# Strassen on the second MLP product of a fused vision-tower kernel, with one layernorm result moved from VectorE to ScalarE

## The chip, the core and the metric

The kernel runs on one core of a Trainium2 chip. The core has a matrix engine (TensorE, written PE), three engines for elementwise work (VectorE or DVE, ScalarE or ACT, GpSimd or POOL), a queue engine (SyncE or SP), an on-chip memory (SBUF), and a small memory into which PE alone accumulates and which the other engines read (PSUM[...]). Each engine works through its own list of instructions in order; semaphores hold an instruction back until what it depends on is done. The metric is the device time of one execution in microseconds (us), lower is better.

## What is computed

The reference, cut to what matters here. Everything is fp32. There are 16384 tokens of 256 features, which the kernel works through in 32 blocks of 512 tokens.

```python
h = tokenizer(x, L0_tok_W)                    # patches, rfft, one matmul: (tokens, 256)
x = layernorm(h)                              # "the first layernorm's result", needed for the residual
# --- attention layer (retention) on x
g = layernorm(x, ln1_g, ln1_b)
q, k, v = g @ Wq.T + bq, g @ Wk.T + bk, g @ Wv.T + bv
mem_t = decay * mem_(t-1) + k_t * v_t         # a scan over the tokens
x = x + q * mem
h2 = layernorm(x, ln2_g, ln2_b)
mlp = relu(h2 @ W1.T + b1) @ W2.T + b2        # 256 -> 1024 -> 256; the second product is changed
h = h + x + mlp
# --- mixture of experts on layernorm(h): 8 experts, each token goes to 2 of them
tok = layernorm(h)
logits = tok @ router_w.T                     # softmax, top 2
h = h + tok + sum over the 2 experts e of share_e * (gelu(tok @ w1[e] + b1[e]) @ w2[e] + b2[e])
```

## The kernel before

Three blocks are in work at once: in one pass of the main loop the newest block (`new`) is embedded and goes through retention, the one before it (`mid`) goes through the MLP, and the one before that (`old`) is routed to its experts. Between these parts stand "slots": in each slot one tile of 256 tokens of some expert is worked on (`enter` is its first matrix product, `leave` its second, `sums` the scaling and the scatter of its result). The order of the instructions on PE, DVE, ACT and SP is that in which the program gives them.

```python
p_mm = ... tile_pool(name="p_mm", bufs=4, PSUM)    # 4 buffers of one bank
p_tm = ... tile_pool(name="p_tm", bufs=3, PSUM)    # 3 buffers
p_sm = ... tile_pool(name="p_sm", bufs=1, PSUM)    # 1 buffer
...
class Norm:
    def apply(self, dst, src, i=0):                # (src - mean) * rstd, on DVE
        for t in range(TT):                        # TT = 4
            nc.vector.tensor_scalar(dst[:, t, :D], src[:, t, :], self.mv[:, t, 0:1],
                                    self.rstd[:, i, t : t + 1], ALU.subtract, ALU.mult)
...
def embed(self):                                   # the end of it
    ...
    norm.factors(twice=True)                       # rstd, on GpSimd
    yield
    self.z = one.tile([P, TT, D], F32, name="z")
    self.zz = one.tile([P, TT, D], F32, name="zz")
    norm.apply(self.zz, self.h, 1)                 # both layernorms in one
    norm.apply(self.z, self.h, 0)                  # the first layernorm, for the residual
...
def residual(self):
    norm = Norm()
    for u in range(U):                             # U = 2
        ps = p_tm.tile([P, 2, D], F32, name="tm")
        ...                                        # 4 transposes of ret into ps, on PE
        nc.vector.tensor_tensor(self.z[:, ts(u, 2), :], ps, self.z[:, ts(u, 2), :], ALU.add)
        for i in range(2):
            norm.stats(self.z, 2 * u + i)
    norm.factors_here()                            # rstd, on DVE: small operations
    self.zz = one.tile([P, TT, D], F32, name="zz")
    norm.apply(self.zz, self.z)
...
def mlp_out(self, u, between=None):
    if u == 0:
        self.norm = Norm()
    ps = p_tm.tile([P, 2, D], F32, name="tm")
    for i in range(2):
        if i and between:
            between()
        for k in range(KH):                        # KH = 8
            nc.tensor.matmul(ps[:, i, :], lhsT=self.aT[:, k, ts(u * 2 + i, P)], rhs=w2_sb[:, k, :],
                             start=k == 0, stop=k == KH - 1)
    nc.vector.tensor_tensor(self.h[:, ts(u, 2), :], ps, self.h[:, ts(u, 2), :], ALU.add)
    for i in range(2):
        self.norm.stats(self.h, u * 2 + i)
    if u == U - 1:
        self.norm.factors_here() if self.i >= NS - 1 else self.norm.factors()
        self.tok = one.tile([P, TT, D], F32, name="tok")
        self.norm.apply(self.tok, self.h)
        ...
...
def sums(self):                                    # of an expert's tile
    ...                                            # 2 small operations for its share
    nc.vector.tensor_tensor(y, ps, bias, ALU.add)  # reads the p_tm buffer of leave
    for c in range(2):
        nc.vector.tensor_scalar(y[:, c, :], y[:, c, :], share[:, c : c + 1], None, ALU.mult)
    ...                                            # scatter-add by GpSimd's DMA queue
...
# the second part of one pass of the main loop
for m in range(KH):
    mid.mlp_in(m)                                  # relu(h2 @ W1.T + b1): aT
    if m == 1:
        new.split1()                               # zz to 16-bit planes, for a transposing DMA
    if m == TT - 1:
        slot(known)
    if m == KH - 3:
        blocks[i + 1].differences(xs.pop(i + 1))
        new.features1()                            # hT, for retention
for t in range(TT):
    old.logits(t)
for m in range(KD):                                # KD = 2
    new.retention(m)
    if old and m == 0:
        old.choose()
take(old.i + 1, old, old.place())                  # routing: small operations on DVE
...
slot(known)
mid.mlp_out(0)
new.residual()
slot(known)
new.split2()
mid.mlp_out(1)
# then the next pass: embed, slot, mlp_in of the next block
```

Of the kernel before, what the change touches and what calls it, by code (L numbers as in the profile page):

```python
# [12 lines left out]
F32 = mybir.dt.float32  # L13
I32 = mybir.dt.int32
# [21 lines left out]
def vit_tower_kernel(  # L36
# [21 lines left out]
    KD, KH = D // P, H // P  # L58
    J = STRIDE // 2
# [90 lines left out]
    w2_sb = const.tile([P, KH, D], F32)  # L150
    nc.sync.dma_start(out=w2_sb, in_=w2.rearrange("(k p) d -> p k d", p=P))
# [157 lines left out]
    class Block:  # L309
# [32 lines left out]
        def embed(self):  # L342
# [40 lines left out]
            self.z = one.tile([P, TT, D], F32, name="z")  # L383
            self.zz = one.tile([P, TT, D], F32, name="zz")
            norm.apply(self.zz, self.h, 1)
            norm.apply(self.z, self.h, 0)

        def split1(self):
            if self.i < EARLY:
                return  # L390
            self.turn = Turn()
            self.turn.split(self.zz)

# [89 lines left out]

        def mlp_out(self, u, between=None):
            if u == 0:
                self.norm = Norm()
            ps = p_tm.tile([P, 2, D], F32, name="tm")
            for i in range(2):
                if i and between:
                    between()  # L490
                for k in range(KH):
                    nc.tensor.matmul(  # L492
                        ps[:, i, :],
                        lhsT=self.aT[:, k, ts(u * 2 + i, P)],
                        rhs=w2_sb[:, k, :],
                        start=k == 0,
                        stop=k == KH - 1,
                    )
            nc.vector.tensor_tensor(self.h[:, ts(u, 2), :], ps, self.h[:, ts(u, 2), :], ALU.add)
            for i in range(2):  # L500
                self.norm.stats(self.h, u * 2 + i)
            if u == U - 1:
                self.norm.factors_here() if self.i >= NS - 1 else self.norm.factors()
                self.tok = one.tile([P, TT, D], F32, name="tok")
                self.norm.apply(self.tok, self.h)
                if self.i == NS:
                    nc.vector.tensor_tensor(self.h, self.h, self.tok, ALU.add)
                    return
                mean, rstd = self.norm.mv[:, :, 0], self.norm.rstd[:, 0, :]
                self.by = small.tile([P, 2, TT], F32, name="by")  # L510
                nc.vector.tensor_scalar(self.by[:, 0, :], rstd, 1.0, None, ALU.add)
# [672 lines left out]
```

## Time and profile before

| | |
|---|---|
| time, median of 3 runs | 2197.89 us (2197.12 to 2201.64) |
| span of the profiled execution | 2216.1 us |
| mean granted PE clock | 0.991 of full speed |
| PE busy | 98% of the span |
| DVE busy | 74% |
| ACT busy | 37% |
| POOL busy | 39% |
| chain of work that ended last | 88% of it on PE |

The profile is of one execution on the chip. A group is a set of instructions of one line, engine and operation, with the time that they were busy, the mean of one in nanoseconds, and the idle time of the engine before them with what ended it. A timeline gives instructions in order of time, neighbours of one kind merged: start, duration, engine, line, operation, what is written from what, how many, and in square brackets the idle time before and its releaser. PE's matmuls overlap in their ends, so the distance of their starts tells their pace, and the duration of one doesn't. LDWEIGHTS is the loading of a matmul's stationary operand.

### The profile page before, as it was taken

Reading aid. Unit: us, or ns where it says so; the run is one execution under the profiler, and the core shown is the slowest. Engines: PE = TensorE matmul, PEld = TensorE weight load, DVE = VectorE, ACT = ScalarE, POOL = GpSimd, SP = SyncE. Lnnn points to the kernel's source line nnn. Section 1 sums busy time; section 2 is a strip of 40 time slices with the busy share of each in tenths; the row PEclk is TensorE's granted clock in tenths of the full one; section 3 lists DMA queues with packets and bytes.
Section 4 is the critical chain, followed back from the end, with each engine's and each line's share of the span. In section 5 each row is a group of like instructions: output and inputs, shape, how many; then the busy total and the mean of one; then the engine's idle time right before and its main releaser. Section 6 shows DMA issues by size and latency. Waiting matters only on the chain.

```text
span 2216.1 us, 28920 instructions
## 1 busy us (share of the span) xinstructions
PE 2161.2 (98%) x8548; PEld 1544.3 (70%) x8548; DVE 1650.9 (74%) x5150; ACT 825.6 (37%) x1329; POOL 873.1 (39%) x760
## 2 busy tenths in 40 slices
PE   8999999999999999999999999999999999998999
PEld 6666666667676667777666777666677766676676
DVE  6678877778778777877877777777787777766454
ACT  1223323444334443432444432344443334442443
POOL 0022243344444434444434444443444444344444
PEclk9999999999999999999999999999999999999999
DMA  3022265676565677657567656665765666588743
GB/s 135 20 97 75 79 147 125 134 163 122 127 149 135 143 139 150 125 129 155 129 139 149 135 128 135 149 136 132 163 130 130 138 146 137 115 172 205 116 66 45
DMA packets 425389, 284.95 MB, mean 129 GB/s; under 512 B 355216, under 2 KB 391056, under 8 KB 421136
## 3 DMA queue, kind: packets, MB, share of 16 engines
q1 hardware_dynamic: 374304, 210.21, 41.4%
q0 software_dynamic: 49632, 67.39, 16.1%
q10 hardware_dynamic: 1296, 5.52, 1.0%
q8 instruction: 67, 1.10, 0.2%
q14 instruction: 90, 0.74, 0.1%
HBM read 118.36 MB, written 88.39 MB: 93 GB/s over the span
## 4 chain that ended last, share of the span: by engine, by line
PE 88%; DVE 3%; DMA 3%; ACT 3%; issue 2%; another core or an unknown queue 0%; POOL 0%; ACTq 0%; DVEq 0%; SPq 0%; POOLq 0%
PE mm L298 31%; PE tm L492 19%; PE tm L353 11%; PE mm L799 9%; PE tm L816 9%; DMA turned<-planes 3%; PE sm L557 2%; PE tm L888 1%; PE tm L451 1%; PE mm L871 1%; PE mm L131 1%; PE mm L265 1%; ACT h L518 1%; ACT row L533 1%; ACT hT L292 1%
## 5 line engine op out<-in xcount | busy, mean ns | idle before, releaser
L839 POOL DMA_INDIRECT out<-y,xg x262 | 429.3, 1638 | 501.0 <-DVE y L835 225.9
L492 PE MATMUL tm<-w_sb,aT 128*128 128x256 f32 x2048 | 462.3, 380 | 16.5 <-issue 14.6
L298 PE MATMUL mm<-hT,w_sb 128*128 128x512 f32 x1024 | 455.4, 596 | 10.7 <-ACT ge L807 5.7
L492 PEld LDWEIGHTS tm<-w_sb,aT 128*128 128x128 f32 x2048 | 387.2, 190 | 80.8 <-issue 27.1
L298 PEld LDWEIGHTS mm<-hT,w_sb 128*128 128x128 f32 x1024 | 193.9, 191 | 232.6 <-issue 207.6
L298 PE MATMUL mm<-hT,wqkv_sb 128*128 128x512 f32 x768 | 342.5, 602 | 4.2 <-DVE hT L292 4.2
L640 POOL DMA_INDIRECT xbuf<-row,to x248 | 242.3, 977 | 258.8 <-DVE full L699 182.4
L807 ACT ACTIVATE ge<-mm,w 128x256 f32<-128x256 f32 x262 | 109.3, 469 | 574.3 <-issue 525.8
L353 PE MATMUL tm<-wu,xv 128*128 128x256 f32 x1280 | 284.8, 381 | 0.0
L298 PEld LDWEIGHTS mm<-hT,wqkv_sb 128*128 128x128 f32 x768 | 145.3, 192 | 176.4 <-issue 160.4
L353 PEld LDWEIGHTS tm<-wu,xv 128*128 128x128 f32 x1280 | 244.3, 191 | 33.3
L799 PE MATMUL mm<-xT,w 128*128 128x256 f32 x1048 | 251.3, 383 | 1.5 <-DVE tile_share L828 1.5
L816 PE MATMUL tm<-w,ge 128*128 128x256 f32 x1048 | 247.6, 379 | 0.9 <-DVE y L833 0.9
L482 ACT ACTIVATE aT<-mm,vec 128x512 f32<-128x512 f32 x256 | 169.9, 684 | 173.7 <-PE mm L298 170.5
L799 PEld LDWEIGHTS mm<-xT,w 128*128 128x128 f32 x1048 | 195.6, 191 | 38.6 <-issue 13.1
L816 PEld LDWEIGHTS tm<-w,ge 128*128 128x128 f32 x1048 | 199.0, 190 | 31.3 <-issue 3.4
L792 ACT COPY xT<-xh 128x512 uint16<-128x512 uint16 x262 | 181.2, 761 | 5.4 <-DMA xh<-xbuf 5.3
L243 POOL TENSOR_SCALAR rstd<-mv 128x4 f32<-128x4 f32 x62 | 41.6, 671 | 319.2 <-DVE mv L224 317.3
L833 DVE TENSOR_TENSOR y<-tm,w 128x512 f32<-128x512 f32 x131 | 90.6, 692 | 70.5 <-PE tm L816 69.7
L416 ACT ACTIVATE ks<-mm,vec 128x512 f32<-128x512 f32 x64 | 44.0, 687 | 248.6 <-PE mm L298 248.6
L597 POOL TENSOR_TENSOR ex<-euler,second 128x4 f32<-128x4 f32 x32 | 34.7, 1084 | 247.1 <-DVE second L589 247.1
L418 DVE SCALAR_TENSOR_TENSOR kv<-mm,vec,ks 128x512 f32<-128x512 f32 x64 | 47.9, 748 | 108.9 <-PE mm L298 108.9
(155 smaller groups left out, 2498.2 us busy)
## 6 DMA issues: line engine op xcount, KB each, us to landing
w<-in_wex SPq DMA_DIRECT2D x113, 641.5 KB
xb<-in_x SPq DMA_DIRECT2D x32, 1040.0 KB
out<-h SPq DMA_DIRECT2D x31, 512.0 KB
bank<-in_wex ACTq DMA_DIRECT2D x8, 641.5 KB
out<-y,xg POOLq DMA_INDIRECT x262
xbuf<-row,to POOLq DMA_INDIRECT x248
xh<-xbuf SPq DMA_TRANSPOSE x131
xg<-xbuf SPq DMA_DIRECT2D x131, 4.0 KB
```

Source lines behind the costliest of these rows:

```text
L298: nc.tensor.matmul(ps, lhsT=w[:, k, ts(m, P)], rhs=rhs[:, k, :], start=k == 0, stop=k == KD - 1)
L353: nc.tensor.matmul(ps[:, n, :], lhsT=xv[:, i, j, :], rhs=wu[:, i, j, :], start=j == 0, stop=j == J - 1)
L418: nc.vector.scalar_tensor_tensor(own_order(self.kv[:, m, :]), tiles_order(pv), vec[:, BV + m : BV + m + 1], own_order(ks), ALU.add, ALU.mult,)
L482: nc.scalar.activation(self.aT[:, m, :], ps, AF.Relu, bias=vec[:, MB1 + m : MB1 + m + 1])
L492: nc.tensor.matmul(ps[:, i, :], lhsT=self.aT[:, k, ts(u * 2 + i, P)], rhs=w2_sb[:, k, :], start=k == 0, stop=k == KH - 1,)
L640: write = nc.gpsimd.indirect_dma_start(out=xbuf, out_offset=bass.IndirectOffsetOnAxis(ap=to[:, c, t : t + 1], axis=0), in_=self.row[:, t, ...
L792: nc.scalar.copy(halves[:, :, :, 1 - i], self.xh[:, i * KD : (i + 1) * KD, :])
L799: nc.tensor.matmul(ps[:, m, :], lhsT=self.w[:, k * D + m * P : k * D + (m + 1) * P], rhs=self.xT[:, k, :], start=k == 0, stop=k == KD - 1,)
L807: nc.scalar.activation(self.ge[:, m, :], ps[:, m, :], AF.Gelu, bias=self.w[:, 5 * D + m : 5 * D + m + 1])
L816: nc.tensor.matmul(ps[:, c, :], lhsT=self.ge[:, k, ts(c, P)], rhs=w[:, (2 + k) * D : (3 + k) * D], start=k == 0, stop=k == KD - 1,)
L833: nc.vector.tensor_tensor(y, ps, w[:, 4 * D : 5 * D].unsqueeze(1).to_broadcast([P, 2, D]), ALU.add)
L839: add = nc.gpsimd.indirect_dma_start(out=out, out_offset=bass.IndirectOffsetOnAxis(ap=self.xg[:, c, NUMBER - D : NUMBER - D + 1], axis=0), ...
```

## The change

The second MLP product, for one block, is a (512 x 1024) times (1024 x 256) product. It is cut into quarters: the activations A into A11, A12 (first 256 tokens) and A21, A22 (last 256), each with half of the 1024 inner columns; the weights B into B11, B12, B21, B22. The plain way needs eight products of quarters. The change uses Winograd's form of Strassen's method with seven: A11 B11, A12 B21, A22 T4, S2 T2, S1 T1, S3 T3, S4 B22. The combinations T1 to T4 of the weights are formed once. The combinations S1 to S4 of the activations are formed by DVE in each block, and the seven results are added into the four quarters of `h`. Its purpose is to take one eighth of this product's multiplications from PE.

So that DVE gets something back, the first layernorm's result for the residual (`z`) is computed by ACT, as scale times `h` plus bias. To make room in SBUF some buffers are made single (`row`, `past`, `table_f`), and the S combinations lie in buffers of other tiles that are free at that time.

The diff, cut to its core:

```diff
-    w2_sb = const.tile([P, KH, D], F32)
+    w2_sb = const.tile([P, 7, KQ, P], F32)        # KQ = 4
...
-            self.z = one.tile([P, TT, D], F32, name="z")
             self.zz = one.tile([P, TT, D], F32, name="zz")
             norm.apply(self.zz, self.h, 1)
-            norm.apply(self.z, self.h, 0)
+            self.norm1 = norm
...
+        def result1(self):
+            mean, rstd = self.norm1.mv[:, :, 0], self.norm1.rstd[:, 0, :]
+            less = small.tile([P, TT], F32, name="less")
+            nc.vector.scalar_tensor_tensor(less, mean, -1.0, rstd, ALU.mult, ALU.mult)
+            self.z = one.tile([P, TT, D], F32, name="z")
+            for t in range(TT):
+                nc.scalar.activation(self.z[:, t, :], self.h[:, t, :], AF.Identity,
+                                     bias=less[:, t : t + 1], scale=rstd[:, t : t + 1])
...
+        def combine1(self):
+            self.A11, self.A12 = [self.aT[:, i * KQ : (i + 1) * KQ, : BLK // 2] for i in range(2)]
+            self.A21, self.A22 = [self.aT[:, i * KQ : (i + 1) * KQ, BLK // 2 :] for i in range(2)]
+            shape = [P, KQ, BLK // 2]
+            self.S1 = one.tile(shape, F32, name="tok")
+            self.S2 = one.tile(shape, F32, name="tokT")
+            self.S3 = self.A21
+            nc.vector.tensor_tensor(self.S1, self.A21, self.A22, ALU.add)
+            nc.vector.tensor_tensor(self.S2, self.S1, self.A11, ALU.subtract)
+            nc.vector.tensor_tensor(self.S3, self.A11, self.A21, ALU.subtract)
+
+        def combine2(self, place):
+            self.S4 = one.tile([P, KQ, BLK // 2], F32, name=place)
+            nc.vector.tensor_tensor(self.S4, self.A12, self.S2, ALU.subtract)
...
+            def product(to, a, b):
+                for i in range(2):
+                    for k in range(KQ):
+                        nc.tensor.matmul(to[:, i, :], lhsT=a[:, k, ts(i, P)], rhs=w2_sb[:, b, k, :],
+                                         start=k == 0, stop=k == KQ - 1)
+            def add(to, what):
+                nc.vector.tensor_tensor(to, to, what, ALU.add)
+            h = self.h.rearrange("p (a i) (c d) -> p a c i d", i=2, d=P)
+            U = self.aT[:, 0, : BLK // 2].rearrange("p (i d) -> p i d", d=P)
             if u == 0:
+                self.ps = p_sm.tile([P, 2, 2, P], F32, name="sm")
+                product(self.ps[:, 0], self.A11, B11)
+                nc.scalar.copy(U, self.ps[:, 0])
+                add(h[:, 0, 0], U)
+                return
+            if u == 1:
+                ps = p_tm.tile([P, 2, 2, P], F32, name="tm")
+                product(ps[:, 0], self.A12, B21)
+                if between:
+                    between()
+                product(ps[:, 1], self.A22, T4)
+                add(h[:, :, 0], ps)
+                return
+            product(self.ps[:, 1], self.S2, T2)
+            add(U, self.ps[:, 1])
+            add(h[:, 0, 1], U)
+            product(self.ps[:, 0], self.S1, T1)
+            add(h[:, :, 1], self.ps[:, 0].unsqueeze(1).to_broadcast([P, 2, 2, P]))
+            if between:
+                between()
+            ps = p_tm.tile([P, 2, 2, P], F32, name="tm")
+            product(ps[:, 0], self.S3, T3)
+            add(U, ps[:, 0])
+            add(h[:, 1], U.unsqueeze(1).to_broadcast([P, 2, 2, P]))
+            product(ps[:, 1], self.S4, B22)
+            add(h[:, 0, 1], ps[:, 1])
+            self.norm = Norm()
+            for t in (2, 3, 0, 1):
+                self.norm.stats(self.h, t)
...
-            self.row = two.tile([P, TT, RW], I32, name="row")
+            self.row = one.tile([P, TT, RW], I32, name="row")
... # the main loop
+                if m == 2:
+                    new.result1()
...
+            if mid:
+                mid.combine1()
             for m in range(KD):
                 new.retention(m)
...
             if old:
                 take(old.i + 1, old, old.place())
+            if mid:
+                mid.combine2("kv")
...
             slot(known)
             if mid:
                 mid.mlp_out(0)
             new.residual()
+            if mid:
+                mid.mlp_out(1)
             slot(known)
...
                 new.split2()
             if mid:
-                mid.mlp_out(1)
+                mid.mlp_out(2)
```

## The prediction

> **What bounds the kernel now.** I read the busy times first, then the groups by line, then one steady block in order of time, on TensorE (PE) and VectorE (DVE). The page's part 1 (busy us, share of the span, instructions):
>
> ```profile
> PE 2161.2 (98%) x8548; PEld 1544.3 (70%) x8548; DVE 1650.9 (74%) x5150; ACT 825.6 (37%) x1329; POOL 873.1 (39%) x760
> ```
>
> PE is busy 98% of the span, and the chain that ended last is 88% PE. So PE sets the end, and DVE seems to have a quarter to spare. That average misleads, as the order of time shows. Groups by line (busy us, mean ns of one, then idle before it):
>
> ```profile
> L492 PE MATMUL tm<-w_sb,aT 128*128 128x256 f32 x2048 | 462.3, 380 | 16.5 <-issue 14.6 <-DVE h L499 1.7
> L492 PEld LDWEIGHTS tm<-w_sb,aT 128*128 128x128 f32 x2048 | 387.2, 190 | 80.8 <-issue 27.1 <-DVE h L499 2.1
> L462 DVE TENSOR_TENSOR h<-h,z 128x1024 f32<-128x1024 f32 x32 | 38.2, 1193 | 0.0
> ```
>
> The first two are the product that is changed: each fp32 matmul leaves two records, so 1024 instructions are 2048. The third gives the price of a DVE addition of 1024 columns. Now one block, the PE's timeline from the start of retention (start, us, operation, count, idle before):
>
> ```profile
> 1011.50 10.54 PE L298 MATMUL mm<-hT,wqkv_sb 128*128 128x512 f32 x24 [0.79 <-DVE hT L292]
> ...
> 1022.23 1.97 PE L799 MATMUL mm<-xT,w 128*128 128x256 f32 x8
> 1024.04 1.89 PE L816 MATMUL tm<-w,ge 128*128 128x256 f32 x8
> 1025.77 7.07 PE L492 MATMUL tm<-w_sb,aT 128*128 128x256 f32 x32
> 1032.68 1.04 PE L451 MATMUL tm<-ident,ret 128*128 128x128 f32 x8
> 1033.55 1.89 PE L799 MATMUL mm<-xT,w 128*128 128x256 f32 x8
> 1035.28 1.89 PE L816 MATMUL tm<-w,ge 128*128 128x256 f32 x8
> 1037.01 7.27 PE L492 MATMUL tm<-w_sb,aT 128*128 128x256 f32 x32
> 1044.11 8.80 PE L353 MATMUL tm<-wu,xv 128*128 128x256 f32 x40
> ```
>
> And DVE in the same stretch:
>
> ```profile
> 1023.25 1.10 DVE L436 SCALAR_TENSOR_TENSOR ret<-mm,vec,ks 128x512 f32<-128x512 f32 x1
> ...
> 1030.21 0.15 DVE L735 TENSOR_TENSOR taken<-taken,upto 1x8 f32<-1x8 f32 x1
> ...
> 1030.65 0.69 DVE L833 TENSOR_TENSOR y<-tm,w 128x512 f32<-128x512 f32 x1
> ...
> 1032.88 0.69 DVE L499 TENSOR_TENSOR h<-tm,h 128x512 f32<-128x512 f32 x1 [0.88 <-PE tm L492]
> ...
> 1041.09 1.38 DVE L252 TENSOR_SCALAR zz<-z,mv,rstd 128x256 f32<-128x256 f32 x4
> ...
> 1050.01 1.38 DVE L252 TENSOR_SCALAR tok<-h,mv,rstd 128x256 f32<-128x256 f32 x4 [3.80 <-POOL rstd L248]
> ```
>
> From 1024.2 to 1030.4 DVE runs the routing of the block before (place and take: about 32 small operations, most near 0.2 us apart). PE doesn't notice, because the first half of the old product (7 us) needs nothing from DVE. From 1034.69 to 1042.47 DVE runs the residual and its layernorm in 7.8 us, and PE again has a slot (3.5) and the second half (7) to chew on. So in this stretch DVE is nearly full and runs one PE stage behind. Its idle time lies elsewhere: 3.3 us at the first `kv`, 3.8 and 1.8 us waiting for GpSimd's `rstd`, 0.9 here. Retention starts follow each other by 65.0 us (361.4 to 1921.1 for 24 blocks), and PE stands idle under 2 us of it.
>
> [...] 32 records of 256 columns from 1025.77 to 1032.68 are 216 ns each; transposes of 128 columns (8 in 0.87 us) are 109 each; and the router's 128x8 matmuls (16 in 1.8) take about 112[...]. [...] The new one puts two products into a bank and reads between them.
>
> **The change, part by part.** *PE.* 32 matmuls of 256 columns a block become 7 x 8 = 56 of 128. Before: 64 records x 216 ns = 13.8 us. After: 112 x 110 (or 112) = 12.3 to 12.5. So 1.4 us a block, 32 blocks, 45 us: the whole prize, and it is 2% of the run.
>
> *DVE.* Added per block: four operand combinations of 1024 columns, 4 x 1.2 = 4.8. The adds of the results: five of 256 columns (0.39 each, as L379) and three of 512 (0.69, L499), 4.0. Removed: two L499 (1.4) and the layernorm's second result (four L252, 1.38), which goes to ACT at about 2 us, with room at 37%. Net about +6 us a block, 190 us in all: DVE would be near 85%.
>
> *Path.* In the built program the waits are: the products of A12 and A22 write the `tm` buffer that the expert's `y` (old L833) must first have read; the S1 product waits for DVE's add of the S2 product (same bank), and the S4 product for the add of the S3 product (same bank). I walk a block from retention's start, times in us, durations from the lines above.
>
> DVE: the `hT` copies end at 0.5, three combinations at 4.1; the first `kv` could start at 3.8, so +0.4. `ret` ends at 13.1 (12.7 before). Place and take, 6.15: 19.25. S4, 1.2: 20.45. Shares 0.35 and `y` 0.7: 21.5. PE meanwhile: slot ends at 14.3, first product (free of `sm` at 14.35) at 16.1, transposes at 17.0. It now needs the `tm` buffer and gets it at 21.55: **4.5 us idle**. The cause is that only 1.8 us of product, not 7, lies there to cover place and take.
>
> PE: two products, 3.5: 25.05; slot, 3.45: 28.5; S2 product, 1.76: 30.3. DVE: `y` scaling 0.6, add 0.4: 22.5; residual 7.75: 30.25; add 0.7, shares and `y` 1.65, then the add that frees the bank 0.4: 33.0. S1 product starts at 33.05: **2.75 idle**. S1 and S3 end at 36.55; drain and one add about 0.6 later the last product starts, **0.6 idle**, and ends at 38.9. The old kernel starts the embedding at 32.6: the new one **6.3 later**, although it did 1.4 us less work.
>
> Behind it nothing gives this back. Four stats now all follow the last add (2.2 instead of 1.1 us), GpSimd's 3.8 us follows, so `tok` slips by 6.8 and the next layernorm with it; PE's own work from the embedding to the next retention is unchanged at 31.1. Next retention: about 38.9 + 31.1 + 1 = 71 instead of 65.0. **+6 us x 25 full blocks = +150.** The four blocks before them (periods of 51 to 58 us, no or few experts to fill PE) lose more at the same waits, some 7 each: +28. The tail, with expert steps between the parts: about 0 to +5. Sum: 2198 + 150 + 28 + 3 = 2379; some of the slip may be absorbed, so I say **2370**.
>
> **Rivals.** *PE stays the bound.* DVE has 25% idle and GpSimd waits could shrink as DVE falls behind; then 2198 - 45 = 2150. For it: PE at 98%, DVE at 74%. Against: the idle time isn't where the new work is; from retention to the last add DVE has almost none. *Only the bank round trips cost.* If DVE kept up, two stalls of about 0.6 us a block eat 40 of the 45 us: 2195. It needs the 4.5 us stall to be absent, which takes DVE being 4 us earlier. *Weight loading doesn't hide.* [...] Against: with 256 columns the loads lie wholly under the matmuls; transposes at 109 have a shorter load (141 against 190 ns), so they prove it only in part. The point of no gain is 13.8/112 = 123 ns.
>
> **Range and chances.** The walk needs two stalls with firm causes; even half of each makes +2 us a block after the saving, 2250. The upper side holds more waits that I didn't see, and early blocks worse than thought. Range 2290 to 2440. Faster by over 2% (below 2154) needs PE to stay the bound entirely: 0.03. Within 2%: 0.07. Slower: 0.90.
>
> **What would show it.** Right: PE busy drops by some 45 us or more while the span grows; in a steady block PE idles 4 to 5 us before the A12 product with DVE `y` as releaser, 2 to 3 before S1 and 0.6 before S4 with DVE `aT` adds; retention's distance is near 71; DVE near 1840 busy. Wrong: records of the 128-column product further apart than 115 ns, block distance below 66, or the PE wait ended by ACT or DMA rather than DVE.

## The result, and the profile after

The changed kernel takes 2398.22 us (median of 4 runs, 2391.55 to 2403.06); before took 2198.14 beside it (2197.12 to 2201.64). The ratio is 1.0905, with a 95% interval of 1.0876 to 1.0934. It is slower by 9%, inside the predicted range of 2290 to 2440 and 28 us above the predicted 2370.

Part 1 of the page after (busy us, share of the span, instructions), and the first line of its chain of work that ended last:

```profile
PE 2196.2 (92%) x10084; PEld 1622.2 (68%) x10084; DVE 1838.6 (77%) x5378; ACT 904.6 (38%) x1489; POOL 918.6 (38%) x760
...
PE 51%; DVE 42%; issue 3%; POOL 1%; DMA 1%; ACT 1%; DVEq 0%; SPq 0%; ACTq 0%; POOLq 0%
```

DVE carried 3% of the chain before and carries 42% now, at a busy share that rose only from 74% to 77%. PE does an eighth less of the product and is yet busy 35 us longer (2161.2 before). Both need the order of time. The PE timeline of one steady block, from the start of retention (start, us, operation, count, idle before and its releaser; A11 lies at 1127.55):

```profile
1112.90 10.55 PE L311 MATMUL mm<-hT,wqkv_sb 128*128 128x512 f32 x24
...
1134.47 5.47 PE L534 MATMUL tm<-w_sb,aT 128*128 128x128 f32 x32 [4.03 <-DVE y L908]
...
1145.76 2.05 PE L534 MATMUL sm<-w_sb,tok 128*128 128x128 f32 x16 [0.57 <-DVE aT L543]
...
1150.11 2.05 PE L534 MATMUL tm<-w_sb,kv 128*128 128x128 f32 x16 [0.51 <-DVE aT L543]
1152.00 8.80 PE L366 MATMUL tm<-wu,xv 128*128 128x256 f32 x40
```

The three stalls of the prediction are there: 4.03 before A12 and A22 (both merged in the second line), 0.57 before S1, 0.51 before S4. The embedding, last line, starts 39.1 after retention; in the block of before that the prediction shows it was 32.6. Over the 25 full blocks the means are 39.2 and 33.4. DVE in the same stretch:

```profile
1125.19 1.10 DVE L463 SCALAR_TENSOR_TENSOR ret<-mm,vec,ks 128x512 f32<-128x512 f32 x1
...
1132.25 1.21 DVE L525 TENSOR_TENSOR kv<-aT,tokT 128x1024 f32<-128x1024 f32 x1
...
1133.73 0.69 DVE L908 TENSOR_TENSOR y<-tm,w 128x512 f32<-128x512 f32 x1
...
1145.29 0.41 DVE L543 TENSOR_TENSOR aT<-aT,sm 128x256 f32<-128x256 f32 x1
...
1156.24 1.38 DVE L265 TENSOR_SCALAR tok<-h,mv,rstd 128x256 f32<-128x256 f32 x4 [1.49 <-POOL rstd L261]
```

None of the first four has a wait in brackets: DVE goes through routing, S4 (the `kv` line, in that buffer), `y`, residual and the adds without a gap, and the add at 1145.29, which frees the S1 bank, comes when the list has come so far. The second stall is shorter than predicted because A12 and A22 took 5.3 us from start to start of the next product, not 3.6. The view by stretches (us; busy us of PE, PEld, DVE, ACT, POOL with instructions; PE clock; DMA share; GB/s) of the stall and the time right behind it:

```profile
1130.20:1134.40 4.20, 0.24 (x3) 0.01 (x1) 3.92 (x16) 1.10 (x2) 3.48 (x3) 1.00 0.40 94
1134.40:1138.50 4.10, 4.03 (x23) 4.03 (x24) 3.89 (x13) 0.00 (x0) 2.99 (x4) 0.64 0.57 226
```

The clock granted to PE is 1.00 in the stall and 0.64 behind it; in steps of 1 us it is 0.50 from 1136.4 to 1138.4 and 1.00 again from 1139.4. A stall of 4.03 us with half clock behind it comes once a block, and the mean clock of the run went from 0.991 to 0.963. The records of 128 columns follow each other by 112 ns in the median at full clock and by 213 at half. So PE's busy time grew through slower matmuls, not through more work: the records are more, but half as wide. In the waits of PE over the whole run (us in total, times, longest) the order is the same:

```profile
PE tm L534 <- DVE y L908: 104.5, 26, 4.0
PE sm L534 <- DVE aT L543: 32.2, 32, 4.7
```

By stages, from the starts of retention in both traces, in us:

| stage | before | after | difference |
|---|---|---|---|
| to the first retention | 37.9 | 39.2 | +1.3 |
| five early distances | 258.2 | 299.1 | +40.9 |
| 25 full blocks (65.0 and 70.25 each) | 1625.0 | 1756.3 | +131.3 |
| the distance behind them | 69.7 | 75.9 | +6.2 |
| rest | 225.3 | 219.1 | -6.2 |
| span of the profiled execution | 2216.1 | 2389.5 | +173.5 |

The profiled execution of before was 18 us above its median and that of the changed kernel 7 below, so the table's 173 is less than the 200 us between the medians.

### The profile page after: what moved, and what is told of

It reads as the page before. It is cut to its first block, busy times and chain, and to the rows that moved or that the text cites. A ratio compares the mean times of both kernels' runs of the same rounds, so it can differ in the third digit from the quotient of the medians.

```text
span 2389.5 us, 32641 instructions
## 1 busy us (share of the span) xinstructions
PE 2196.2 (92%) x10084; PEld 1622.2 (68%) x10084; DVE 1838.6 (77%) x5378; ACT 904.6 (38%) x1489; POOL 918.6 (38%) x760
## 4 chain that ended last, share of the span: by engine, by line
PE 51%; DVE 42%; issue 3%; POOL 1%; DMA 1%; ACT 1%; DVEq 0%; SPq 0%; ACTq 0%; POOLq 0%
PE tm L366 11%; PE mm L311 11%; PE tm L534 8%; PE mm L874 6%; PE tm L891 6%; PE sm L534 4%; DVE ks L453 3%; DVE xv L343 3%; DVE xv L340 3%; DVE ret L463 3%; DVE y L908 2%; DVE kv L445 2%; DVE st L236 2%; DVE y L910 2%; DVE hT L305 1%
## 5 line engine op out<-in xcount | busy, mean ns | idle before, releaser
L914 POOL DMA_INDIRECT out<-y,xg x262 | 439.3, 1677 | 439.5 <-DMA out<-y,xg 185.4
L715 POOL DMA_INDIRECT xbuf<-row,to x248 | 276.0, 1113 | 258.8 <-DVE full L774 175.5
L311 PEld LDWEIGHTS mm<-hT,w_sb 128*128 128x128 f32 x1024 | 195.4, 191 | 219.1 <-issue 213.4
L534 PE MATMUL tm<-w_sb,aT 128*128 128x128 f32 x1536 | 236.4, 324 | 104.5 <-DVE y L908 104.5
L534 PEld LDWEIGHTS tm<-w_sb,aT 128*128 128x128 f32 x1536 | 228.6, 239 | 110.7 <-DVE y L908 110.6
L874 PEld LDWEIGHTS mm<-xT,w 128*128 128x128 f32 x1048 | 195.2, 191 | 39.2 <-issue 16.1
L891 PEld LDWEIGHTS tm<-w,ge 128*128 128x128 f32 x1048 | 199.5, 190 | 31.4 <-issue 3.3
L375 ACT COPY ab<-tm 128x512 f32<-128x512 f32 x32 | 18.7, 586 | 370.9 <-PE tm L366 370.9
```

The costliest lines, as they stand in the source:

```text
L311: nc.tensor.matmul(ps, lhsT=w[:, k, ts(m, P)], rhs=rhs[:, k, :], start=k == 0, stop=k == KD - 1)
L534: nc.tensor.matmul(to[:, i, :], lhsT=a[:, k, ts(i, P)], rhs=w2_sb[:, b, k, :], start=k == 0, stop=k == KQ - 1,)
L715: write = nc.gpsimd.indirect_dma_start(out=xbuf, out_offset=bass.IndirectOffsetOnAxis(ap=to[:, c, t : t + 1], axis=0), in_=self.row[:, t, ...
L874: nc.tensor.matmul(ps[:, m, :], lhsT=self.w[:, k * D + m * P : k * D + (m + 1) * P], rhs=self.xT[:, k, :], start=k == 0, stop=k == KD - 1,)
L891: nc.tensor.matmul(ps[:, c, :], lhsT=self.ge[:, k, ts(c, P)], rhs=w[:, (2 + k) * D : (3 + k) * D], start=k == 0, stop=k == KD - 1,)
L914: add = nc.gpsimd.indirect_dma_start(out=out, out_offset=bass.IndirectOffsetOnAxis(ap=self.xg[:, c, NUMBER - D : NUMBER - D + 1], axis=0), ...
```

## The experiments

All ratios are to the kernel before, run on the same chip, where it took 2205 to 2211 us; one of e5's executions, 3267 us at a clock of 0.647, is left out. "Distance" is the mean of the full blocks. Theory L, named in the expectations, is the prediction's: DVE works through its list without a gap from the last `ret` to the add that frees the S1 bank, and this sets the distance of blocks. W says that DVE's total busy time counts, C that PE's half clock is what costs.

| run | what | time, us | ratio and interval | distance, us |
|---|---|---|---|---|
| e1_take_late | after, routing moved late | 2651.92 | 1.1997, 1.1959 to 1.2034 | 79.5 |
| e2_tm4 | after, a fourth `tm` buffer | 2439.12 | 1.1036, 1.1008 to 1.1065 | 71.7 |
| e3_seven_eighths | before, 1/8 of the product left out | 2195.84 | 0.9938, 0.9913 to 0.9962 | 64.7 |
| e4_combos_only | before, plus S1 to S4 unused | 2245.81 | 1.0164, 1.0135 to 1.0193 | 65.9 |
| e5_z_alone | before, `z` by ACT | 2214.46 | 1.0029, 1.0014 to 1.0043 | 64.6 |
| e9_strassen_alone | after, `z` by DVE | 2403.52 | 1.0868, 1.0837 to 1.0899 | 70.9 |
| e6_banks | after, banks not shared | 2322.32 | 1.0515, 1.0491 to 1.0539 | 68.3 |
| e7_banks_tm4 | both e6 and e2 | 2301.37 | 1.0415, 1.0391 to 1.0438 | 67.6 |
| e8_fill | after, dummy work in the stall | 2458.79 | 1.1124, 1.1098 to 1.115 | 72.5 |
| e10_no_combos | e7 without S1 to S4 | 2376.39 | 1.0753, 1.0726 to 1.078 | 69.9 |
| e11_no_combos_banks | after without S1 to S4 | 2451.85 | 1.1108, 1.1075 to 1.1141 | 72.0 |
| e12_fixed_places | e10 with fixed places for the rows | 2194.47 | 0.9953, 0.9937 to 0.997 | 63.5 |

### The parts of the change: e5, e9, e4, e3

**e5** makes only the second part of the change (`z` by ACT) in the kernel before; **e9** takes it out of the changed kernel.

```diff
# e5, on before                               # e9, on after: the reverse
-            norm.apply(self.z, self.h, 0)
+            self.norm1 = norm
+        def result1(self): ...    # scale * h + bias, four on ACT
+                if m == 2:
+                    new.result1()
```

> The second part of the change alone: the kernel before, with the first layernorm's result for the residual computed by ACT (four activations) instead of DVE. DVE loses 1.4 us a block, ACT gains about 2. Theory L (DVE's order decides): the operations that go stand behind the one that the next transposing transfer waits for and in front of an expert's `y`, so little of the 1.4 us is on a path: 0 to -0.5 us a block, 0 to -15 us in all, a ratio of 0.993 to 1.0. Rival W (the sum of DVE work counts): -1.4 x 32 = -45 us, ratio 0.98.

> The changed kernel with only the first part of the change: z is made by DVE again. DVE loses the 1.38 us a block that it had got back, but between the first layernorm's rstd and retention, where DVE waits for PE before the first kv. Theory L (the DVE list from the last ret to the add that frees the S1 bank sets the distance of blocks): nothing of that stretch changes, so 1.085 to 1.10 times before, and the waits of PE before the A12 product stay at 4.0. Rival (DVE's total busy time sets the time): 32 x 1.38 = 44 us slower than the changed kernel, 1.11.

e5 is 0.3% slower than before, a little outside L's range, so the second part by itself brings nothing here. e9 at 1.0868 can't be told from the changed kernel's 1.0905, as L expected; 44 us of DVE work given back in a place where DVE waits for PE anyway (before the first `kv`) are worth next to nothing. So the loss is the Strassen part's. The trace of e9 differs in one more thing: some 70 completion signals of PE come over 1 us late, in every full block (what such a signal is, e3 and e10 show), its second `y` comes 0.7 us later, and the embedding starts 39.9 after retention instead of 39.2, which is the whole difference in distance.

**e4** adds the four combinations to before, in the places where the changed kernel has them, with nobody reading them: by the estimate in the expectation 149 us of DVE work (DVE's busy time rose by 131), PE unchanged.

```diff
+        def combine1(self):        # S1, S2, S3 of aT's quarters, into tok, tokT, tok
+        def combine2(self, place): # S4 into kv
...
+            if mid:
+                mid.combine1()
             for m in range(KD):
                 new.retention(m)
...
+            if mid:
+                mid.combine2("kv")
```

> The kernel before, plus the four combinations S1 to S4 on DVE at the places of the changed kernel (three before retention, one behind the routing), unused: 4.8 us of DVE work a block, nothing else changed. Theory L (a place where PE has 7 us of product to cover it costs little): about 0.4 to 1.0 us a block, 2210 to 2235 us. Rival W (the sum of DVE work counts): 4.8 x 31 = 149 us, 2345.

Measured are +35 us, 0.9 a block, which is inside L's range; W falls. As long as PE has the old product to work on, most of this DVE time is absorbed. The 0.9 us don't lie in the stretch that L is about, though: from retention to the embedding e4 needs 32.7 us (before 33.4), and from there to the next retention 33.2 (31.6). The transposing DMA there is issued 37.0 us after retention instead of 35.8, which is the path that e3 shows next.

**e3** leaves the last eighth of the inner dimension out of the second MLP product of before (k = 7 of 8). It takes 4 of the 32 matmuls of 256 columns from PE in each block, 4 x 2 records x 216 ns = 1.73 us, in 32 blocks 55 us, and adds nothing anywhere.

```diff
-                for k in range(KH):
+                for k in range(KH - 1):
```

> The kernel before, with the last eighth of the inner dimension of the second MLP product left out (28 matmuls of 256 columns a block instead of 32; the output lacks that part). It shows what taking an eighth from PE is worth when DVE has nothing more to do: 4 x 0.432 x 32 = 55 us. Theory L: PE bounds the kernel before, so nearly all of it comes: 2148 us (2138 to 2165). Rival: DVE was already the bound, and it comes out between 2180 and 2198.

This missed: 14 us gained of 55. So what I took for granted, that PE sets the end before, holds only to a part. The means of the 25 full blocks show where the gain goes. The embedding starts 31.3 us after retention, 2.2 earlier than before, so in front of it the whole time of the left-out matmuls is gained. From the embedding to the next retention e3 needs 33.4 us where before needs 31.6, and most of the gain is lost again. The waits of PE name what came up:

```profile
PE mm L298 <- ACT ge L807: 29.3, 24, 1.2
```

In one of e3's blocks (retention at 938.83), DVE, ACT and SP's queue in order of time, and then PE:

```profile
967.30 1.51 DVE L252 TENSOR_SCALAR zz<-z,mv,rstd 128x256 f32<-128x256 f32 x4
968.03 0.84 ACT L807 ACTIVATE ge<-mm,w 128x256 f32<-128x256 f32 x2 [14.29 <-issue]
...
968.85 1.99 ACT L278 COPY planes<-zz 128x1024 uint16<-128x1024 uint16 x2
...
974.20 3.25 SPq L286 DMA_TRANSPOSE turned<-planes  x1
...
980.27 2.64 ACT L292 COPY hT<-turned 128x512 uint16<-128x512 uint16 x4 [5.78 <-DMA turned<-planes]
```

```profile
988.74 1.98 PE L298 MATMUL mm<-hT,w_sb 128*128 128x512 f32 x4 [1.08 <-ACT ge L807]
```

The copies of `planes` start as soon as DVE's `zz` is there and are done at 970.84. The transposing DMA that turns them is issued only at 974.20, because SP works in order and tile loads stand in front of it, the last at 973.70. Counted from retention's start that is 35.4 us, and 35.6 in the mean of 24 blocks, hardly earlier than before's 35.8, although PE is 2.2 us ahead. ACT's `hT` waits for it, the next `ge` on ACT's list comes behind `hT`, and PE waits for that `ge`. So before has a second limit close behind PE, which runs through SP's queue.

The `ge` at 968.03 shows something else. The expert's product that it reads ends at 961.91, and PE's completion signal for it is in the trace's semaphore events at 967.96, 6 us late. In this block hardly anything had to wait for that, since `planes` starts right at the end of `zz`. The same delay is in the trace of before: the product shown in the prediction at 1033.55 ends at 1035.44, and its `ge` starts at 1042.13. I come back to it with e10.

### The waits of PE: e2, e6, e7, e8, e1

**e2** gives the `tm` pool a fourth buffer, taken from `mm`, so that A12 needn't wait for `y`.

```diff
-    p_mm = ... bufs=4      p_tm = ... bufs=3
+    p_mm = ... bufs=3      p_tm = ... bufs=4
```

> The changed kernel with four `tm` buffers in PSUM instead of three (and three `mm` instead of four). The wait of PE for `y` was a wait for a `tm` buffer. Rival B (PSUM buffers are the cause): the 4.0 us wait goes and 100 us come back, about 2300. Theory L: the wait for `y` goes, but the S1 product still waits for the same add at the end of DVE's list, so that wait grows from 0.6 to about 4 to 5 us and the embedding starts where it did, 39 us after retention's start: 2385 to 2445, the upper part if the PE clock then halves in the last products instead of in the A12 product.

PE's timeline at S1 in one block (retention starts at 1061.86):

```profile
1094.55 3.78 PE L534 MATMUL sm<-w_sb,tok 128*128 128x128 f32 x16 [6.51 <-DVE aT L543]
```

A12 and A22, at 1079.06, have no wait and full clock (1.00 from 1078.9 to 1083.9). S1 starts 32.69 after retention, where the changed kernel has 32.86: the wait has moved from one product to another, and the add of DVE that ends it comes at the same time. This is the plainest support for L. And the kernel became slower, not equal: now the 6.5 us stall is followed by S1 at half clock (0.50 in the mean from 1091.9 to 1095.9; 3.6 us for 16 records that take 1.8), and nothing hides this, because the next thing behind is the embedding.

**e8** tries the opposite: the stall before A12 stays, but PE gets 3.4 us of dummy matmuls in it, to keep its clock.

```diff
+                if old and at["enter"]:
+                    dummy = p_mm.tile([P, BLK], F32, name="mm")
+                    for _ in range(4):
+                        nc.tensor.matmul(dummy, lhsT=w1_sb[:, 0, :P], rhs=mid.hT[:, 0, :], start=True, stop=True)
                 mid.mlp_out(1)
```

> The changed kernel with four extra matmuls of 512 columns (3.4 us, results unused) in front of the A12 product of each block that has slots, where PE idles 4 us for `y`. PE then isn't idle there, so its clock shouldn't fall to half afterwards (it is 0.64 on average in the 4.1 us after that idle time, and the product takes 5.3 us instead of 3.5). Theory C (the clock is a cost of its own): the 1.8 us come back in each block: -45 us, ratio 1.07. Theory L: the product is faster, but S1 then waits 1.8 us longer for the same add of DVE; nothing changes: 2390 to 2405, ratio 1.085 to 1.093.

Both expectations missed. PE's timeline (retention at 1069.82), then the stretch behind S1's wait, with columns as above:

```profile
1091.22 3.84 PE L534 MATMUL tm<-w_sb,aT 128*128 128x128 f32 x32 [0.60 <-DVE y L908]
...
1103.18 3.58 PE L534 MATMUL sm<-w_sb,tok 128*128 128x128 f32 x16 [2.89 <-DVE aT L543]
```

```profile
1103.80:1107.80 4.00, 4.00 (x26) 4.00 (x26) 0.69 (x1) 0.00 (x0) 2.92 (x2) 0.67 1.03 238
```

A12 is fast again, so S1 waits 2.89 instead of 0.57, and now the half clock (0.67 in the mean) falls behind S1. In the changed kernel the half clock sits before DVE's add and is mostly hidden: it lasts 3.4 us in 15 of the 25 full blocks (mean distance 69.9) and 6.8 us in the other ten (70.7). Where it comes after the last wait it costs about 1.8 us a block: from the start of S1 to the embedding the changed kernel takes 6.2 us, e2 8.0 and e8 8.1 (means of the full blocks). S1 itself starts within 0.4 us of the changed kernel's 33.0 in both (32.7 and 33.4). That e8's S1 is the later one comes with its second `y`, 0.6 us later than in the changed kernel: in this block it stood 0.63 us behind a late signal of PE, for a product that had ended at 1098.51, and started at 1101.46.

**e6** takes the bank round trips away: S1 and S4 share one `tm` buffer, S3 goes into the `sm` buffer, all adds come after the products, and the statistics of the four token groups are taken in their order. **e7** is e6 with e2's fourth buffer.

```diff
             product(self.ps[:, 1], self.S2, T2)
-            add(U, self.ps[:, 1]); add(h[:, 0, 1], U)
-            product(self.ps[:, 0], self.S1, T1)
-            ...
+            product(ps[:, 0], self.S1, T1)       # ps: a tm buffer
+            product(ps[:, 1], self.S4, B22)
+            add(U, self.ps[:, 1]); add(h[:, 0, 1], U)
+            product(self.ps[:, 0], self.S3, T3)
+            ...                                  # the adds of S1, S4, S3
```

> The changed kernel with the products laid out so that no PSUM bank is read by DVE while PE still has to write its other half: S1 and S4 share a `tm` buffer and are read when both are there, S3 goes into `sm` behind S2. Same work, same adds. The waits of PE for DVE's `aT` adds (0.57 and 0.51 us in a steady block) go. Theory L: PE still waits 4 us for the `y`; then it runs the last four products without a stop, and DVE is free of its three waits for PE there (1.7, 1.1 and 1.4 us): the embedding starts 37 to 37.5 us after retention's start instead of 39.1, the distance of blocks falls from 70.1 to about 68.5: 2350 to 2370, ratio 1.065 to 1.075. Rival B (the bank round trips are the whole loss): 2200 or less.

> e6_banks with four `tm` buffers and three `mm` buffers: now neither a bank nor a `tm` buffer holds PE in this stretch, and what is left is DVE's list itself. Theory L: PE's wait for `y` goes (the embedding can start at 31 to 33), but DVE reaches the last stats only some 2 to 3 us later in the block than in the kernel before, and that goes on to the layernorms and to the next `hT`: distance of blocks 66 to 67.5, ratio 1.01 to 1.03. Rival B (PSUM was the cause, PE is the bound): PE's 45 us are now earned: ratio 0.975 to 0.98.

e6 did better than expected: 1.9 us a block and about half of the early blocks' loss (their five distances are 47.0, 52.2, 58.9, 60.3, 61.9, together 280.4; in the changed kernel 47.0, 59.7, 61.7, 63.0, 67.7, together 299.1, and in before 258.2). Its 4.03 us wait for `y` is as before, and the embedding starts 37.2 after retention. e7 removes that one too, but less came of it than expected. Its timeline (retention at 998.66):

```profile
1015.80 3.74 PE L534 MATMUL tm<-w_sb,aT 128*128 128x128 f32 x32
...
1031.28 2.05 PE L534 MATMUL sm<-w_sb,aT 128*128 128x128 f32 x16 [2.93 <-DVE aT L543]
```

Again the wait moved down the list, to the last product, which needs the add of S2's result out of its bank. The embedding is at 34.5 here and at 35.2 on the average; behind it PE needs 32.4 us to the next retention instead of 31.0, since it now waits for ACT's `ge` there. The kernel is still 4% behind before.

**e1** moved the routing (`take`) behind the last statistics of the MLP, into the gap where DVE waits for GpSimd's `rstd`, to make `y` early.

```diff
-                take(old.i + 1, old, old.place())
+                writes = old.place()
...
+            def routing():
+                take(old.i + 1, old, writes)
+                advance("load", ...)
-                mid.mlp_out(2)
+                mid.mlp_out(2, routing=routing)     # between factors() and tok
```

> The changed kernel, with one thing moved: the part of the routing that makes the table of tiles (take, 3.6 us of small DVE operations) no longer stands between the last `ret` and the expert's `y`, but behind the last add of the MLP, in the time in which DVE waits for GpSimd's rstd. Same work, same slots. Theory L (DVE's list from `ret` to the add that frees the bank of the S1 product has no gap, and sets the distance of the blocks): the 4.0 us wait of PE for `y` shrinks to about 1, the embedding starts some 3.4 us earlier in the block (35.7 instead of 39.1 after retention's start), DVE gives part of it back at `tok`, and the distance of blocks falls from 70.1 to 67 or 68: about 2320 us (2285 to 2345). Rival W (what counts is the sum of the work added to DVE, wherever it lies): the sum is unchanged, so 2390 to 2400.

It missed by far: 79.5 us a block. Most of the wait for `y` went (13.4 us in total are left of 104.5), but S1's grew to 165.2 over 32 times, and S1 starts 32.6 us after retention, hardly earlier than the changed kernel's 33.0. In one block (retention at 1149.38):

```profile
1178.24 1.56 POOL L916 DMA_INDIRECT out<-y,xg  x1 [0.30 <-issue]
...
1180.19 0.69 DVE L910 TENSOR_TENSOR y<-tm,w 128x512 f32<-128x512 f32 x1 [3.47 <-remote]
```

DVE is free for its second `y` 3.5 us earlier, as L said, and then waits as long. The product that this `y` reads had ended at 1174.50; PE's signal for it came at 1180.16, 0.4 us after the last of a run of indirect transfers on GpSimd. So late signals of PE, which e10 shows at large, stand here as a second limit right behind DVE's list. Behind the embedding, DVE waits 190.5 us in total, 28 times, for `turned`, which transposing DMAs write, and PE needs 38.4 us to the next retention instead of 31.0. The tile loads share SP's queue with those DMAs and wait there for the table of tiles (475.9 us in total, 27 times); that they hold the DMAs up is my reading. So the run is no clean test of L. It suggests too that the place of routing is tied to the DMA queue.

### What is left when DVE is taken out: e10, e11, e12

**e10** and **e11** leave the four combinations out of e7 and of the changed kernel; quarters of `aT` stand in their place, so the MLP's result isn't the reference's. PE and the adds are as they were.

```diff
-            nc.vector.tensor_tensor(self.S1, self.A21, self.A22, ALU.add)
-            ...                                   # S2, S3, S4
+            self.S1, self.S2, self.S3, self.S4 = self.A22, self.A22, self.A21, self.A12
```

> e7_banks_tm4 with the four operand combinations left out (quarters of aT stand in their place, so the MLP's result isn't the reference's). 4.8 us of DVE a block go. Theory L: three of the four lie before the first kv, where DVE waits for PE anyway, so 0.4 of them counted, and S4 counts whole with its 1.2: 1.6 us a block off the path, 67.4 to about 65.8, 1.01 to 1.03 times before. Rival B (DVE's total busy time): 4.8 us a block, 0.97. Rival P (PE with its 128-column products and waits bounds e7): unchanged at 1.04.

> The changed kernel, its PSUM buffers as they are, with the four operand combinations left out in the same way. Theory L: 1.6 us a block off DVE's list before y, so the wait before the A12 product falls from 4.0 to about 2.4 and the distance from 70.2 to about 68.6: 1.06 to 1.075 times before. [...] Rival (bank and buffer waits alone make the loss): 1.09 as before.

Neither theory had this: with 4.8 us a block less for DVE to do, both became slower, e10 by 3.4 points against e7 and e11 by 2 against the changed kernel. In e11 the wait before A12 fell, as L said, from 4.03 to 2.9 (2.4 expected). But something else came: in one block DVE then stood 2.28 us before the add of A12's and A22's products, which had ended at 1090.80 and were signalled at 1096.45. In e10 PE carries 87% of the chain, and its largest wait has no releaser: 108.9 us in 148 pieces, in products that go into the `sm` buffer. PE's timeline in one block, then ACT's, and the first and the last of GpSimd's transfers:

```profile
1051.42 1.89 PE L867 MATMUL mm<-xT,w 128*128 128x256 f32 x8
...
1054.87 0.72 PE L527 MATMUL sm<-w_sb,aT 128*128 128x128 f32 x5
...
1060.28 0.60 PE L527 MATMUL sm<-w_sb,aT 128*128 128x128 f32 x2 [1.90 <-issue]
1061.79 1.24 PE L527 MATMUL sm<-w_sb,aT 128*128 128x128 f32 x5 [0.91 <-issue]
```

```profile
1062.05 0.84 ACT L875 ACTIVATE ge<-mm,w 128x256 f32<-128x256 f32 x2 [13.15 <-issue]
```

```profile
1047.18 1.07 POOL L708 DMA_INDIRECT xbuf<-row,to  x1 [6.50 <-DVE full L767]
...
1059.39 1.67 POOL L907 DMA_INDIRECT out<-y,xg  x1 [0.30 <-issue]
```

The S2 product of 1.8 us takes 8, in drops, without any wait; and the `ge` of the product that ended at 1053.31 starts at 1062.05. PE's semaphore events show it whole: matmul groups that end at 1051.58, 1053.31 and 1055.04 all signal between 1061.88 and 1062.06. In 24 of the 25 full blocks three signals are held so, by 6.8 to 10.3 us. GpSimd meanwhile issues ten indirect transfers in a row, eight of a block's rows to their experts' places and two of results, one every 1.3 to 1.9 us, from 1047.2 to 1061.06. The signals come 0.8 us after the end of the last, in block after block. The fetching of instructions doesn't explain it: in the trace of before the signals that are over 1 us late come at 69 points of time, 68 of them within 1.7 us behind the end of an indirect transfer on GpSimd, but anywhere from 0.2 to 34.2 us behind the last packet of a fetch. What GpSimd does in such an interval isn't shown; the run of them is what stands alongside.

**e12** tests this. The rows get fixed places, 128 of every block to each expert, and so go in two plain transfers instead of eight indirect ones. The routing isn't the reference's; PE, DVE and ACT do the work of e10.

```diff
-            for t in range(TT):
-                for c in range(2):
-                    write = nc.gpsimd.indirect_dma_start(out=xbuf, out_offset=...(to[:, c, t : t + 1]), in_=self.row[:, t, :], ...)
+            places = xbuf[: E * REG, :].rearrange("(t c r) d -> r t c d", t=TT, c=2)
+            for c in range(2):
+                write = nc.gpsimd.dma_start(out=places[self.i * P : (self.i + 1) * P, :, c, :], in_=self.row)
```

> e10_no_combos with fixed places for the routed rows: each block's 512 rows go as 128 to every expert, so the eight indirect transfers that GpSimd issues in a row (1.3 us apart) become two plain ones. PE, DVE and ACT do the same work; the routing isn't the reference's. Of e10 the trace shows PE's completion signals held back by 7 to 10 us in nearly every block and released 0.8 us after the last of GpSimd's ten indirect transfers, and PE standing 4 to 6 us without a wait in the same stretch. Theory G (the run of indirect transfers is what holds PE up): both go, the distance of blocks falls from 70 to 65 or 66, 0.99 to 1.02 times before. Rival (PE holds itself up with 128-column products back to back): nothing changes, 1.07. Rival (the bytes of the rows hold it up, which move as before): at most a little better, 1.05 to 1.07.

By the ratios its time is 7.4% below e10's and even 0.5% below that of before. GpSimd's timeline and PE's in one block:

```profile
971.55 1.68 POOL L710 DMA_DIRECT2D xbuf<-row  x2 [6.17 <-DVE whole L765]
```

```profile
979.54 1.95 PE L527 MATMUL sm<-w_sb,aT 128*128 128x128 f32 x16
...
986.19 2.05 PE L527 MATMUL sm<-w_sb,aT 128*128 128x128 f32 x16 [1.13 <-DVE aT L536]
```

The S2 product is whole again, hardly a signal is late (4 over 1 us in the run, 96 in e10), and the distances are 63.4 to 63.6 in every full block but the first. So what e12 changed did away with what held PE up in e10. But e12 changed several things at once: of what kind the transfers are and how many, where the rows land and how early, and that all experts fill evenly; which of them does it isn't separated. And the run of transfers by itself isn't enough: in the trace of the changed kernel the same ten stand in every full block, 16.5 to 31.4 us after retention, and no signal is late.

## Why the prediction was right, step by step

**"PE sets the end ... 45 us: the whole prize."** This is the step that failed, though the forecast of a slower kernel didn't rest on it. PE was busy 98% before, but e3 took 55 us from PE and got 14, because another chain, through SP's queue, `hT` and `ge`, stands close behind PE. The arithmetic of PE's own work was right: 112 records of 112 ns, 12.5 us, instead of 64 of 216, 13.8. e12's 63.5 us a block, 1.5 below before, look like the predicted 1.4 but don't show it: the best stages of before, 32.4 to the embedding and 31.0 behind it, add up to 63.4 as well, and e12's edit wasn't tried on before. So in the kernel as it stands most of the prize isn't there to be had, even without a DVE cost. A high busy share of PE said that little time was idle, not that less PE work would shorten the run.

**The pace of 110 to 112 ns** for a 128-column record held: 112 in the median wherever the clock is full. The rival that loads wouldn't hide behind streams falls.

**"PE busy drops by some 45 us"** was wrong in sign: it rose by 35. The step left out the clock, which is at half for 3.4 to 6.8 us behind each 4 us stall. An estimate from the mean clocks and the spans: 0.9% of 2216 us, 20, were lost before, and 3.7% of 2389.5, 88, after; these 68 us are most of the 80 by which the step is off.

**DVE:** predicted near 1840 busy, measured 1838.6. The "near 85%" beside it divides this by the old span; by the predicted 2370 it is 78%, and 77% was measured.

**The walk through a block:** A12's stall 4.5 predicted, 4.03 measured; S4's 0.6 and 0.51; S1's 2.75 and 0.57. This last was mis-sized, and only in its form: the half clock fills the difference. Stall, slow product and stall come to 4.03 + 1.8 + 0.57 = 6.4, against the 7.25 of the two predicted stalls; the S1 product started 32.86 after retention (33.05 predicted), the embedding 39.1 (38.9). e2 and e8 show that S1's start hardly depends on where PE waits.

**The distance:** 71 predicted, 70.25 measured. The prediction's block of before was one of the quickest to the embedding; over the full blocks the embedding moved by 5.8 us, from 33.4 to 39.2, and not by 6.3. Behind it PE runs to the next retention without a wait, 31.0 us in 24 of the 25 blocks, where before needs 31.6 on the average; the further 1 us that the prediction added there didn't come. `tok` slipped by some 4.7 us instead of 6.8, with a shorter wait for GpSimd's `rstd` (1.49 instead of 3.8), but nothing on PE waited for it. Over 25 blocks that is +131 instead of +150. **The early blocks** were mis-sized the other way, +41 instead of +28; e6 gets 19 of the 41 back, so the bank round trips are about half of it. The one distance behind the full blocks lost 6, and the rest, where 0 to +5 was predicted, gave back 6, so the sum is nearer to the forecast than its terms are.

**The rivals.** "PE stays the bound" (2150) falls. "Only the bank round trips cost" (2195) falls as stated, but the round trips weighed more than the "0.6 us" twice: removing them (e6, with its other changes of order) took 3.9 points of the 9.

**What the walk couldn't see.** The wait behind the waits of this stretch, PE's late signals while GpSimd issues the rows, was in the trace of before, and I had not looked for it. In the recorded trace of the changed kernel no signal is late by more than 0.02 us, so its 70.25 us rest on DVE's list, and e2's S1, which starts where the changed kernel's does, agrees. But with DVE relieved (e1, e10, e11) the late signals come up behind it, and the loss stays. They are also in e9 (some 70 over 1 us), e6 (62), e7 (58) and e2 (36). So of the 9 points about 4 went with the bank round trips and 1 more with the fourth buffer; how the 4 that e7 keeps divide between DVE's list, late signals and the chain through `ge` stays open. Whether the changed kernel, or before, would gain from e12's edit alone wasn't tried.

No version here that has the Strassen product and the whole computation beats before: the best, e7, is at 1.0415.

## What to carry to other kernels

An in-order engine that is 75% busy can still have no gap in one stretch, and a change that shortens PE's work there takes away the cover under which that list ran; walk the stretch engine by engine before counting a saving. Before counting on a saving at all, leave the work out and time it: a free eighth of the product was worth 14 us of 55, and this one run would have shown how little there was to win. When a wait is removed, look where it goes, and whether anything behind it still hides what it brings with it.

## What the runs showed of the hardware that I had not expected

The half clock of PE after a stall of some 4 us costs little or much by its place: the same few slow microseconds were mostly hidden before DVE's add in the changed kernel and lay on the path behind it in e2 and e8, with 1.8 us a block. In e8 a 2.89 us wait was enough, with the clock at 0.90 in the stretch of the wait and 0.67 behind it; in the block of e7 shown above, a 2.93 us wait was followed by a clock of 1.00. So the length of the wait alone doesn't tell it here.

In several of these traces PE's completion signals come up to 10 us late, and in e10 PE itself stands still without a wait, while GpSimd issues a run of indirect transfers. In before, 103 signals of 1182 come over 1 us late and 31 over 4 us; in e10, 96 and 81 of 1252; in e12, 4 and none; in the changed kernel, with the same run of transfers, none. A profile shows it only as "issue" or as a late consumer, so it has to be looked for by setting a matmul's end beside the start of what reads it. What holds the signals, whether the recording of the profile has a part in it, and why the trace of the changed kernel shows none of it, is open.
